# A graph layer's second aggregation with the operands of its matmuls exchanged, and gate logits on VectorE

## The chip, the cores and the metric

The kernel runs on one core of a Trainium2 chip. A core has TensorE (PE in the profile, with its weight loads as PEld), VectorE (DVE), ScalarE (ACT), GpSimd (POOL) and SyncE (SP); TensorE writes its results to PSUM (this kernel takes it in tiles of up to 512 fp32 values per partition, called banks here), and the other engines bring them to SBUF. The metric is the device time of one execution in microseconds (us), lower is better; the time before is the median of three runs.

## The reference: what is computed

6250 nodes with 256 features. `x` is normalised per row to `xn`. Three things are added to `x`: a graph network of two convolutions on `xn`, a linear attention on `xn`, and then, on the normalised sum, a mixture of experts with 8 experts of which each row uses 2. What matters here:

```python
def _graph_conv(x, edges, W0, b0, W1, b1):
    agg = segment_sum(x[src], dst, N_NODES) / deg[:, None]     # deg: edges into a node, at least 1
    return x @ W0 + b0 + agg @ W1 + b1
...
x = x + graph_network(xn) + linear_attention(xn)
x_flat = _layernorm(x)
gate_logits = x_flat @ Wg + bg + bias                          # 256 x 8
topk_vals, topk_idx = jax.lax.top_k(gate_logits, 2)
topk_w = softmax(topk_vals)
out = x + sum over the two chosen experts of topk_w * expert(x_flat)
```

The second convolution multiplies by its weight first and aggregates afterwards: the sum over a node's neighbours runs over rows of 256 values.

## The kernel before

Nodes are cut into NB = 49 blocks of 128 rows, and blocks into NGRP = 13 groups of T = 4 (the last has one block). Aggregation is a product with the adjacency matrix, built tile by tile. A step (g, j) in `steps` takes the edges from block j into the blocks of group g: 13 x 49 = 637 steps. `sent[:, j]` holds block j's rows to be summed, as a high and a low part (`k` = 0 and 1) in the fp32r format, 2 x 256 values per row.

Stages, in order of time:

1. Edges are sorted into `place`, while the rows of `x` are normalised.
2. The first pass (`aggregate`): for each step the adjacency tile is built from one-hots (L649, L668), copied to SBUF in fp32r (L671) and in bf16 (L679), and the latter is written to `adjd` in DRAM. `products` (L619 to L628) multiplies.
3. A dense stage makes `btab` (all that is added to a row besides the second aggregation) and the new `sent`.
4. **The second pass** (L931 to L1113), where the change lies.
5. The experts: 105 tiles of 128 rows (L1170 to L1286).

In the second pass each step needs the tile of adjacency in fp32r. SP reloads it from `adjd` in batches of JL = 7 steps (`reload`, L804, tile `many`, two buffers), and `widen` (L940) casts one step's part, on ScalarE in odd steps (L946) and on VectorE in even ones (L948), to one of five buffers of `adj2`. Then `products` issues four matmuls: stationary is one half (c) of the high or low rows, 128x128, moving is the adjacency, 128x512. So the sums, two banks per group, have a feature per partition and a node per column.

When a group's 49 steps are done, `gate(g)` (L951 to L1095) works on its four blocks. It is a generator in pieces; each `next(running)` issues one piece between steps of the next group, so that its work lies beside that group's matmuls. Its pieces, in order:

- load `btab` rows (L956), copy the two sums to `agT` (L959 on VectorE, L960 on ScalarE);
- per block: two transposes (L970) give rows again, L972 multiplies by 1/degree and adds `btab`; then the row's mean and variance (L975, L976);
- the standard deviation on ScalarE (L978), its reciprocal (L980), the normalised rows (L983), and GpSimd's copies of them (L986 to L988);
- transposes of the rows into `yT` (L994, copies L996), 16 matmuls with the gate's weight `wg` (L1005), and the bias (L1007): the logits `lg`;
- the two best experts and their weights (L1014 to L1055), with two small matmuls that count places (L1046, L1048), and the places (L1057 to L1079);
- GpSimd writes the rows to the experts' `lists` (L1085).

PE, VectorE and ScalarE execute their instructions in the order of the program here (`manual_schedule`); SP and GpSimd are left to a scheduler. The order is set by the loop at L1097: with AH = 4, the cast of step t stands before the products of step t - 4.

The constants of the gate are loaded at L895 to L900 by SP: `wg`, then `bg2`, which VectorE adds (L900).

Of the kernel before, what the change touches and what calls it, by code (L numbers as in the profile page):

```python
# [18 lines left out]
P = 128  # L19
# [14 lines left out]
def bcast_rows(ap, n):  # L34

    return bass.AP(tensor=ap.tensor, offset=ap.offset, ap=[[0, P], [1, n]])
# [3 lines left out]
def tile_gps_layer(ctx: ExitStack, tc: tile.TileContext, a, out):  # L40
# [578 lines left out]
    def products(pg, sums, adj, g, j):  # L619

        n = len(blocks(g))
        if j == 0:
            sums[g] = [pg.tile([P, T * P], F32, name=f"sum{c}") for c in range(DC)]
        for c in range(DC):
            for k in range(2):
                nc.tensor.matmul(sums[g][c][:, :n * P], sent[:, j, k, c * P:(c + 1) * P],  # L626
                                 adj[:, :n * P], start=(j == 0 and k == 0),
                                 stop=(j == NB - 1 and k == 1))  # L628
# [265 lines left out]
    gc = ctx.enter_context(tc.tile_pool(name="gate", bufs=1))  # L894
    wg = gc.tile([P, DC, NE], F32, name="wg")  # L895
    nc.sync.dma_start(wg, a["Wg"].rearrange("(c p) e -> p c e", p=P))
    bg2 = gc.tile([P, 2, NE], F32, name="bg2")
# [33 lines left out]
    with ExitStack() as p3:  # L931
        wk = p3.enter_context(tc.tile_pool(name="work3", bufs=2))
        ap = p3.enter_context(tc.tile_pool(name="adj2", bufs=5))
        pg = p3.enter_context(tc.tile_pool(name="pg2", bufs=2, space=PSUM))
        ps = p3.enter_context(tc.tile_pool(name="ps3", bufs=2, space=PSUM))
        py = p3.enter_context(tc.tile_pool(name="py3", bufs=2, space=PSUM))
        p3.enter_context(tc.manual_schedule(engines={ENG.PE, ENG.DVE, ENG.Activation}))
        adjs, sums = {}, {}

        def widen(t):  # L940
# [8 lines left out]
            adjs[t] = adj  # L949

        def gate(g):  # L951

            bs = blocks(g)
            n = len(bs)
            bt = wk.tile([P, T, D], F32, name="bt3")
            nc.sync.dma_start(  # L956
                bt[:, :n], btab[bs[0] * P:(bs[-1] + 1) * P, :].rearrange("(t p) d -> p t d", p=P))
            agT = wk.tile([P, DC, T * P], F32, name="agT", bufs=1)
            nc.vector.tensor_copy(agT[:, 0, :n * P], sums[g][0][:, :n * P])  # L959
            nc.scalar.copy(agT[:, 1, :n * P], sums[g][1][:, :n * P])  # L960
            yield
            yield
# [3 lines left out]
            rs = wk.tile([P, T], F32, name="rs3")  # L966
            for i, b in enumerate(bs):
                pt = py.tile([P, 512], F32, name="py")
                for c in range(DC):
                    nc.tensor.transpose(pt[:, c * P:(c + 1) * P], agT[:, c, i * P:(i + 1) * P],  # L970
                                        ident)
                nc.vector.scalar_tensor_tensor(bt[:, i], pt[:, :D], rdeg[:, b:b + 1], bt[:, i],  # L972
                                               op0=OP.mult, op1=OP.add)
                yield
                nc.vector.bn_stats(st[:, i, :], bt[:, i])  # L975
                nc.vector.bn_aggr(mv[:, i, :], st[:, i, :])  # L976
                yield
# [11 lines left out]
            yield  # L989
            yT = wk.tile([P, DC, T * P], F32, name="yT", bufs=1)  # L990
            for c in range(DC):
                tp = ps.tile([P, T * P], F32, name="tp")
                for i in range(n):
                    nc.tensor.transpose(tp[:, i * P:(i + 1) * P], rows[:, i, 0, c * P:(c + 1) * P],  # L994
                                        ident)
                nc.scalar.copy(yT[:, c, :n * P], tp[:, :n * P])  # L996
                yield
            yield


            lg = wk.tile([P, T, NE], F32, name="lg")
            pl = py.tile([P, 512], F32, name="py")
            for i in range(n):
                for c in range(DC):
                    nc.tensor.matmul(pl[:, i * NE:(i + 1) * NE], yT[:, c, i * P:(i + 1) * P],  # L1005
                                     wg[:, c, :], start=(c == 0), stop=(c == DC - 1))
            nc.vector.tensor_tensor(lg[:, :n], pl[:, :n * NE].rearrange("p (t e) -> p t e", e=NE),  # L1007
                                    bg[:, None, :].to_broadcast([P, n, NE]), op=OP.add)
            yield
            top = wk.tile([P, 2, T], F32, name="top")  # L1010
# [85 lines left out]

        AH = 4  # L1097
        running = iter(())
        for t in range(len(steps) + AH):
            if t < len(steps):  # L1100
                if steps[t][1] % JL == 0 and steps[t] not in loaded:
                    reload(t)
                widen(t)
            next(running, None)
            if t >= AH:
                g, j = steps[t - AH]
                products(pg, sums, adjs.pop(t - AH), g, j)
                if j == NB - 1:
                    for _ in running:
                        pass  # L1110
                    running = gate(g)
        for _ in running:
            pass  # L1113
# [210 lines left out]
```

## Time and profile before

| what | value |
|---|---|
| median of 3 runs | 2676.82 us (2675.69 to 2680.96) |
| the profiled execution's own time | 2674.58 us |
| its span, first to last instruction | 2672.8 us |
| mean granted clock of TensorE | 0.939 of full speed |
| busy in the span: PE, DVE, ACT, POOL | 92%, 59%, 36%, 13% |
| second pass: first matmul of L626, last matmul of L626 | 1555.2 us, 2191.9 us |
| busy from 1609 to 1660 us (51 us): PE, DVE, ACT, POOL | 51.0, 22.6, 18.9, 9.5 us |
| granted clock there | 1.00 |

A line such as `L948 DVE CAST adj<-many ... x319 | 135.8, 427 | 318.2 <-PE sum L626 254.8` says: the instructions of line 948 on VectorE, 319 of them, write `adj` from `many`; together 135.8 us busy, 427 ns each on average; before them the engine stood idle for 318.2 us in all, and 254.8 of it ended when TensorE had finished something at L626. In an order of time, a line gives the start, the length, the engine and line, and how many instructions were merged; the length of a merged row reaches to the end of its last instruction, so a pitch is the difference of two starts divided by the count. Matmuls are pipelined, so their durations overlap.

### The profile page before, as it was taken

What the parts mean: (1) busy time and instruction counts of PE and PEld (TensorE: products, weight loads), DVE (VectorE), ACT (ScalarE), POOL (GpSimd) and SP (SyncE); (2) the same over time, 40 slices, a digit from 0 to 9 for tenths busy, and PEclk for the clock granted to TensorE, in tenths of its full rate; (3) what the DMA queues carried; (4) which work ended last, traced back from release to release, by engine and by line L of the source; (5) the groups of instructions that cost most, each with busy time, mean ns of one, the idle gap of its engine ahead of it and who ended that gap; (6) DMA issues with size and microseconds to landing.
All of it is one profiled execution on the core that took longest, in us unless ns stands there. A gap on an engine that the chain in (4) does not pass through costs nothing. (4 is left out here: it accounts for less than half of the span.)

```text
span 2672.8 us, 41922 instructions
## 1 busy us (share of the span) xinstructions
PE 2452.5 (92%) x13030; PEld 1815.2 (68%) x13030; DVE 1587.8 (59%) x4247; ACT 951.0 (36%) x2476; POOL 344.6 (13%) x375
## 2 busy tenths in 40 slices
PE   3666769999999999989999989999999987999998
PEld 2455547777777777766677768888888874777665
DVE  5999888888888888721111124444434434666665
ACT  1332225555555555511111123334334322323332
POOL 0000000000000000000000011121121122454444
PEclk7777779999999999979999989999999978999999
DMA  2111613333333333222111154445454433223333
GB/s 75 52 51 52 209 54 109 108 107 107 107 107 107 105 110 108 86 66 83 55 56 55 50 208 150 165 161 168 156 166 162 150 120 96 77 76 103 105 112 96
DMA packets 227535, 286.75 MB, mean 107 GB/s; under 512 B 51798, under 2 KB 199937, under 8 KB 227046
## 3 DMA queue, kind: packets, MB, share of 16 engines
q1 hardware_dynamic: 204386, 241.06, 28.1%
q0 software_dynamic: 17072, 34.33, 3.8%
q10 hardware_dynamic: 5844, 8.58, 0.9%
q8 instruction: 107, 1.75, 0.3%
q14 instruction: 126, 1.03, 0.1%
HBM read 151.43 MB, written 147.10 MB: 112 GB/s over the span
## 5 line engine op out<-in xcount | busy, mean ns | idle before, releaser
L626 PE MATMUL sum<-adj,sent 128*128 128x512 f32 (+1 forms) x5096 | 1332.4, 403 | 10.2 <-DVE blank L918 5.9
L626 PEld LDWEIGHTS sum<-adj,sent 128*128 128x128 f32 x5096 | 907.9, 196 | 161.4 <-issue 6.3
L671 ACT ACTIVATE adj<-pt 128x512 fp32r<-128x512 f32 (+1 forms) x637 | 365.7, 574 | 337.2 <-PE pt L668 335.8
L649 DVE TENSOR_TENSOR oh<-iota,place 128x1024 bf16<-128x1024 bf16 (+1 forms) x686 | 426.7, 628 | 0.3 <-PE pt L668 0.2
L679 DVE CAST kept<-adj 128x512 bf16<-128x512 f32 (+1 forms) x637 | 262.1, 411 | 114.9 <-ACT adj L671 106.6
L946 ACT CAST adj<-many 128x512 fp32r<-128x512 bf16 (+1 forms) x318 | 188.8, 595 | 385.9 <-PE sum L626 345.1
L948 DVE CAST adj<-many 128x512 fp32r<-128x512 bf16 (+1 forms) x319 | 135.8, 427 | 318.2 <-PE sum L626 254.8
L668 PE MATMUL pt<-oh 128*128 128x128 bf16 x2548 | 261.5, 224 | 2.4 <-DVE oh L649 1.8
L668 PEld LDWEIGHTS <-oh 128*128 128x128 bf16 x2548 | 151.1, 99 | 161.8 <-DVE oh L649 131.3
L1226 PEld LDWEIGHTS po<-w2e,hT 128*128 128x128 f32 x840 | 159.4, 190 | 67.3 <-issue 26.3
L1206 PE MATMUL pm<-w1e,yT 128*128 x420 | 200.2, 599 | 1.8 <-DMA row<-lists 1.3
L1226 PE MATMUL po<-w2e,hT 128*128 x840 | 198.5, 379 | 1.0 <-ACT hT L1218 1.0
L1230 ACT ACTIVATE res<-res,row 128x256 f32<-128x256 f32 x105 | 53.3, 508 | 301.3 <-DVE res L1229 152.0
L453 PE MATMUL rt<-carry,route 128*128 128x100 bf16 x931 | 81.8, 265 | 84.5 <-DVE carry L440 65.3
L907 POOL IOTA home_i<- 128x8 int32 x1 | 0.1, 128 | 1158.5 <-DVEq L702 1158.5
L453 PEld LDWEIGHTS <-route 128*128 128x128 bf16 x931 | 73.1, 132 | 94.7 <-issue 84.5
L1085 POOL DMA_INDIRECT lists<-rows,place_i x98 | 97.2, 991 | 298.5 <-DVE rows L1077 265.1
L1262 POOL DMA_INDIRECT out_dram<-both,at x105 | 106.0, 1009 | 161.5 <-DVE both L1260 158.7
L872 DVE TENSOR_TENSOR bt<-bt,pb 128x256 f32<-128x256 f32 x49 | 20.6, 421 | 174.1 <-PE pb L870 174.1
L671 ACT ACTIVATION_READ_ACCUMULATOR adj<-pt 128x1 f32 x637 | 123.9, 194 | 0.0
L1247 POOL DMA_INDIRECT got<-ybuf,at x105 | 108.1, 1030 | 84.5 <-issue 33.0
L1209 DVE TENSOR_TENSOR hb<-pm,b1c 128x512 f32<-128x512 f32 x105 | 72.7, 692 | 64.2 <-PE pm L1206 62.0
(253 smaller groups left out, 2557.4 us busy)
## 6 DMA issues: line engine op xcount, KB each, us to landing
adjd<-kept SPq DMA_DIRECT2D x588, 128.0 KB
many<-adjd SPq DMA_DIRECT2D x84, 896.0 KB
row<-lists SPq DMA_DIRECT2D x105, 130.5 KB
ybuf<-xn SPq DMA_DIRECT2D x1, 13440.0 KB
ybuf<-res SPq DMA_DIRECT2D x105, 128.0 KB
xn<-in_x_dram SPq DMA_DIRECT2D x12, 512.0 KB
xnT_d<-xnT ACTq DMA_DIRECT2D x12, 512.0 KB
xnT<-xnT_d SPq DMA_DIRECT2D x12, 512.0 KB
```

The source lines that it names most:

```text
L453: nc.tensor.matmul(pl[:, r], routes[q // 4][:, q % 4, :, r], carry[:, q - q0, :, :, r], start=(q == 0), stop=(q == Q - 1))
L626: nc.tensor.matmul(sums[g][c][:, :n * P], sent[:, j, k, c * P:(c + 1) * P], adj[:, :n * P], start=(j == 0 and k == 0), stop=(j == NB - 1 a ...
L649: nc.vector.tensor_tensor(oh, iota2[:, None].to_broadcast([P, m, P, 2]), place[:, j, v0:v0 + m, None, :].to_broadcast([P, m, P, 2]), op=OP ...
L668: nc.tensor.matmul(cols, o[:, :, r], o[:, :, 1 - r], start=(m == 0), stop=(m + 1 == len(todo)))
L671: nc.scalar.activation(adj[:, :n * P], pt[:, :n * P], AF.Copy, accum_out=degp[:, j, g:g + 1])
L679: nc.vector.tensor_copy(kept[:, :n * P], adjs[t][:, :n * P].bitcast(F32))
L946: nc.scalar.copy(adj[:, :n * P], from_)
L948: nc.vector.tensor_copy(adj[:, :n * P], from_)
L1206: nc.tensor.matmul(pm, yT[:, c], w1e[:, bass.ds(e, 1), c, :].rearrange("p o f -> p (o f)"), start=(c == 0), stop=(c == DC - 1))
L1226: nc.tensor.matmul(po, hT[:, f], w2e[:, bass.ds(e, 1), f, :].rearrange("p o d -> p (o d)"), start=(f == 0), stop=(f == EC - 1))
L1247: ga = nc.gpsimd.indirect_dma_start(out=gots[t % 4], out_offset=None, in_=ybuf, in_offset=bass.IndirectOffsetOnAxis(ap=outs[t][1][:, 0:1], ...
L1262: st = nc.gpsimd.indirect_dma_start(out=out, out_offset=bass.IndirectOffsetOnAxis(ap=at[:, 1:2], axis=0), in_=both, in_offset=None, bounds ...
```

## The change

In the second pass the stationary operand becomes one 128x128 block of the adjacency tile, and the moving operand is the 512 values of block j's high and low rows together. A product gives one block's sums with a node per partition, the high rows' sum in the left 256 columns and the low rows' sum in the right ones: one PSUM bank per block, four per group, where two banks served a group before. `pg2` has six banks now, and the pool `ps3` is gone.

A new function `received` issues a step's products in place of `products`. During a group's first step (j = 0) it issues only blocks 0 and 1, and in the second step (HOLD = 2) these two and then blocks 2 and 3 of both steps. It also loads the group's `btab` rows in the first step.

`gate` no longer has `agT`: eight scalar_tensor_tensor add the two halves of each block's sum, times 1/degree, to the `btab` rows, and they are issued at once behind the last products of the group. `yT` is gone too: the logits are made on VectorE by eight multiply-and-sum instructions per block, one per expert, over 256 values; two of them are a piece. `wg` holds the whole weight on each partition (2048 values), by a load that repeats it for all 128. AH is 3.

```diff
-    wg = gc.tile([P, DC, NE], F32, name="wg")
-    nc.sync.dma_start(wg, a["Wg"].rearrange("(c p) e -> p c e", p=P))
+    wg = gc.tile([P, D, NE], F32, name="wg")
+    nc.sync.dma_start(wg.rearrange("p d e -> p (d e)"),
+                      bcast_rows(a["Wg"].rearrange("d e -> (d e)"), D * NE))
...
-        pg = p3.enter_context(tc.tile_pool(name="pg2", bufs=2, space=PSUM))
-        ps = p3.enter_context(tc.tile_pool(name="ps3", bufs=2, space=PSUM))
+        pg = p3.enter_context(tc.tile_pool(name="pg2", bufs=6, space=PSUM))
...
+        HOLD = 2
+        def received(t):
+            g, j = steps[t]
+            n = len(blocks(g))
+            if j == 0:
+                bts[g] = wk.tile([P, T, D], F32, name="bt3")
+                nc.sync.dma_start(
+                    bts[g][:, :n], btab[g * T * P:(g * T + n) * P, :].rearrange("(t p) d -> p t d", p=P))
+                sums[g] = []
+            todo = [(t, i) for i in range(n if j >= HOLD else min(n, 2))]
+            if j == HOLD - 1:
+                todo += [(s, i) for i in range(2, n) for s in range(t - HOLD + 1, t + 1)]
+            for s, i in todo:
+                js = steps[s][1]
+                if js == 0:
+                    sums[g].append(pg.tile([P, 2 * D], F32, name="sum"))
+                nc.tensor.matmul(sums[g][i], adjs[s][:, i * P:(i + 1) * P],
+                                 sent[:, js].rearrange("p k d -> p (k d)"),
+                                 start=(js == 0), stop=(js == NB - 1))
...
         def gate(g):
...
-            agT = wk.tile([P, DC, T * P], F32, name="agT", bufs=1)
-            nc.vector.tensor_copy(agT[:, 0, :n * P], sums[g][0][:, :n * P])
-            nc.scalar.copy(agT[:, 1, :n * P], sums[g][1][:, :n * P])
-            yield
+            bt = bts.pop(g)
+            for i, b in enumerate(bs):
+                for k in range(2):
+                    nc.vector.scalar_tensor_tensor(bt[:, i], sums[g][i][:, k * D:(k + 1) * D],
+                                                   rdeg[:, b:b + 1], bt[:, i], op0=OP.mult,
+                                                   op1=OP.add)
             yield
...
-            for i, b in enumerate(bs):
-                pt = py.tile([P, 512], F32, name="py")
-                for c in range(DC):
-                    nc.tensor.transpose(pt[:, c * P:(c + 1) * P], agT[:, c, i * P:(i + 1) * P],
-                                        ident)
-                nc.vector.scalar_tensor_tensor(bt[:, i], pt[:, :D], rdeg[:, b:b + 1], bt[:, i],
-                                               op0=OP.mult, op1=OP.add)
-                yield
+            for i in range(n):
                 nc.vector.bn_stats(st[:, i, :], bt[:, i])
                 nc.vector.bn_aggr(mv[:, i, :], st[:, i, :])
                 yield
...
-            yT = wk.tile([P, DC, T * P], F32, name="yT", bufs=1)
-            for c in range(DC):
-                tp = ps.tile([P, T * P], F32, name="tp")
-                for i in range(n):
-                    nc.tensor.transpose(tp[:, i * P:(i + 1) * P], rows[:, i, 0, c * P:(c + 1) * P],
-                                        ident)
-                nc.scalar.copy(yT[:, c, :n * P], tp[:, :n * P])
-                yield
-            yield
...
             lg = wk.tile([P, T, NE], F32, name="lg")
-            pl = py.tile([P, 512], F32, name="py")
-            for i in range(n):
-                for c in range(DC):
-                    nc.tensor.matmul(pl[:, i * NE:(i + 1) * NE], yT[:, c, i * P:(i + 1) * P],
-                                     wg[:, c, :], start=(c == 0), stop=(c == DC - 1))
-            nc.vector.tensor_tensor(lg[:, :n], pl[:, :n * NE].rearrange("p (t e) -> p t e", e=NE),
-                                    bg[:, None, :].to_broadcast([P, n, NE]), op=OP.add)
-            yield
+            for i in range(n):
+                for e in range(NE):
+                    nc.vector.tensor_tensor_reduce(
+                        out=bt[:, i], in0=rows[:, i, 0, :D], in1=wg[:, :, e], scale=1.0,
+                        scalar=bg[:, e:e + 1], op0=OP.mult, op1=OP.add, accum_out=lg[:, i, e:e + 1])
+                    if e % 2:
+                        yield
...
-        AH = 4
+        AH = 3
...
-                products(pg, sums, adjs.pop(t - AH), g, j)
+                received(t - AH)
                 if j == NB - 1:
                     for _ in running:
                         pass
                     running = gate(g)
+                    next(running)
```

## Prediction

> **What bounds the kernel now.** I read the table of 40 slices first, then the busy time by stretches, then the waits of the second pass, then the order of time on PE and on VectorE inside one group. The second pass runs from 1555 us, the first matmul of L626 after the dense stage, to 2191.9 us. First the costliest groups (out<-in, count | busy us, mean ns | idle before, and what ended it):
>
> ```profile
> L626 PE MATMUL sum<-adj,sent 128*128 128x512 f32 (+1 forms) x5096 | 1332.4, 403 | 10.2 <-DVE blank L918 5.9
> L946 ACT CAST adj<-many 128x512 fp32r<-128x512 bf16 (+1 forms) x318 | 188.8, 595 | 385.9 <-PE sum L626 345.1
> L948 DVE CAST adj<-many 128x512 fp32r<-128x512 bf16 (+1 forms) x319 | 135.8, 427 | 318.2 <-PE sum L626 254.8
> L671 ACT ACTIVATION_READ_ACCUMULATOR adj<-pt 128x1 f32 x637 | 123.9, 194 | 0.0
> ```
>
> Both casts wait for PE to free a buffer, and PE waits almost for nothing: TensorE is the bound. The 403 ns are no cost per matmul, since matmuls overlap; their pitch is read from the order of time on PE over one group (start, length, count):
>
> ```profile
> 1858.53 0.40 PE L970 MATMUL py<-ident,agT 128*128 128x128 f32 x2
> 1858.68 2.10 PE L626 MATMUL sum<-adj,sent 128*128 128x512 f32 x8
> 1860.62 0.38 PE L970 MATMUL py<-ident,agT 128*128 128x128 f32 x2
> ...
> 1872.47 0.60 PE L994 MATMUL tp<-ident,rows 128*128 128x128 f32 x4
> 1872.83 1.19 PE L626 MATMUL sum<-adj,sent 128*128 128x512 f32 x4
> ...
> 1876.17 1.85 PE L1005 MATMUL py<-wg,yT 128*128 128x8 f32 x16
> 1877.87 11.44 PE L626 MATMUL sum<-adj,sent 128*128 128x512 f32 x48
> 1889.14 0.19 PE L1046 MATMUL py<-both,after 128*128 128x32 bf16 x1
> 1889.18 0.18 PE L1048 MATMUL py<-ahead,onesb 128*128 128x32 bf16 x1
> 1889.21 18.91 PE L626 MATMUL sum<-adj,sent 128*128 128x512 f32 x80
> 1907.96 0.66 PE L970 MATMUL py<-ident,agT 128*128 128x128 f32 x2
> ```
>
> From 1889.21 to 1907.96 are 80 matmuls, so one is 0.2345 us and a step of four 0.938. A group's 196 are 46.0 us. The starts of L970 in groups ten apart (1611.26 and 2106.05) give 49.48 us per group. The other 3.5 us are gate(g)'s own PE work, of which L1046 and L1048 (0.08) stay.
>
> **What goes.** agT's transposes (L970), yT's transposes (L994), the logit matmuls (L1005) and their copies: 3.42 us of PE per group. Gates 0 to 10 run inside full groups, so 11 x 3.42 = 37.6 us. The new products are again four matmuls of 512 columns and four weight loads per step, so I keep 0.2345. That operands trade places may shift the pitch: in the first pass the same four take 1.01 us (700.72 to 701.73), 0.2525 each. I hold this as a rival.
>
> **What comes on VectorE.** Per full group: eight scalar_tensor_tensor (STT) in place of two halves of agT's eviction and four STT, and 32 multiply-and-sums (TTR, 256 elements, two fp32 SBUF inputs, a scalar operand, a sum written out). VectorE is busy 20 us of 50, so on average there is room; the order decides. Each step takes a cast (every second one on VectorE) and one piece of the gate; during the 32 TTRs a piece is two TTRs. The adjacency has five buffers, so VectorE cannot work more than four to five steps ahead.
>
> The pitch p of a TTR decides. Rows that bear on it:
>
> ```profile
> L1258 DVE SCALAR_TENSOR_TENSOR both<-row,got x105: 471/479/485, 2243.0 to 2667.2; 128x256 f32<-128x256 f32 x105
> L1152 DVE TENSOR_TENSOR diag<-ident,spec x1: 424/424/424, 2207.6 to 2207.6; 128x256 f32<-128x256 f32 x1
> L918 DVE MEMSET blank<- x1: 59/59/59, 1555.0 to 1555.0; 128x1 f32 x1
> ...
> 1621.32 0.74 DVE L983 TENSOR_SCALAR rows<-bt,mv,rs 128x256 f32<-128x256 f32 x2
> ...
> 2202.70 0.17 DVE L1036 TENSOR_TENSOR both<-pick 128x8 bf16<-128x8 f32 x1
> 2202.93 0.06 DVE L1040 MEMSET both<- 128x4 uint32 x1
> ```
>
> Two independent L983 (0.41 each) take 0.74: neighbours overlap by 0.08. L1040 overwrites what L1036 wrote and starts 0.06 after its end; other dependent neighbours start 0.03 to 0.04 after. All eight TTRs of a block write the same scratch row bt[:, i], so I count 0.04 of wait. Low end: a plain product that overlaps, 0.424 - 0.08 = 0.34. High end: STT 0.479, plus the separate read of a sum that ScalarE shows behind L671 (0.194), plus 0.04, is 0.71. I take STT plus the cheapest VectorE instruction that writes one value per partition (0.059) plus 0.04: **p = 0.58**, because STT has the same operands and the engine is VectorE, not ScalarE.
>
> The weight is read with a step of 32 bytes. Nearest rows: L305, whose int32 input alternates in steps of 76 bytes, takes 313 ns for 304 elements, as L302 does on a plain run, so I add nothing; L152 (34 elements in steps of 100 bytes, 192 ns) is 22 ns longer than L156 (49 elements in a row, 170 ns), at most some 0.9 ns per element, which would be 0.23 us per TTR, p = 0.81.
>
> The Trainium skill (SBUF — State Buffer, Door 1, on 16-byte lines) speaks against the change: each access that crosses into a new line pays a penalty, and here every access does. If that doubled the time per element, p would be an estimated 0.85 and the sum below +125 us; L305 against L302 shows no such price.
>
> **The sum inside a group**, from the end of its predecessor's last matmul, on VectorE: STTs start at -0.5 (they need a finished bank), in four pairs, dependent within a pair: 4 x 0.52 + 3 x 0.40 + 0.40 = 3.7, done at 3.2. Six casts at 0.35: 2.1. Four bn_stats with bn_aggr at 0.63: 2.5. Wait for the square root on ScalarE (table load 1.28 and 0.30, less a cast beside it): 1.3. Reciprocal 0.2, four rows at 0.33: 1.3. That is 10.6 when TTRs begin. Eight pairs of steps follow, each 4p + 0.35. The cast of step 30 is thus ready at 13.4 + 32p, and PE wants it at 29 x 0.938 = 27.2. PE's stall is 32p - 13.8, at least some 0.9 (the cast behind the STTs is late every second group, by 0.85; one bank 0.1; the root on ScalarE before its cast 0.3). With p = 0.58: 4.76 us against 3.42 saved, a net loss of 1.34 a group, 11 x 1.34 = +14.7.
>
> The casts queued behind TTRs are what PE waits for; HOLD covers the evictions, since two spare banks take 4 x 0.2345 = 0.94 us of matmuls and the first pair of STTs is done by 0.5. POOL's copy of rows (L986, 1.04 us) now runs beside TTRs and not transposes; I count nothing for it, or one microsecond a group if it blocks VectorE.
>
> **Group 12** (one block) took 2154.2 to 2191.9, 37.7 us, at 196 short matmuls; now PE needs 49 x 0.2345 = 11.5 and gate(11) is the longer: 3.7 + 2.8 stats + 1.6 root + 1.9 rows + 32p + 6.0 for L1014 to L1077 + 25 casts at 0.18 = 20.5 + 32p = 39.1: +1.4. **Tail**, gate(12): now 13.3 us from the last sum to L1119 (2205.26). Without transposes two STTs 1.05, then 3.24 to rows, 8p, and 4.97 as before: 8p - 4.0 = +0.6.
>
> **Start.** wg grows from 8 KB to 1 MB on SP's queue, ahead of bg, the rows of btab and reloads of many; L900 on VectorE waits for bg, with casts behind it. By stretches (PE, PEld, DVE, ACT, POOL busy, clock, DMA share, GB/s):
>
> ```profile
> 1560.00:1566.00 6.00, 6.00 (x28) 4.82 (x27) 1.28 (x3) 2.23 (x4) 0.17 (x1) 1.00 1.05 398
> 1566.00:1574.00 8.00, 4.27 (x19) 3.10 (x17) 0.30 (x1) 0.58 (x2) 0.00 (x0) 0.92 1.03 401
> ```
>
> Transfers are full here and PE waits 3.9 us for many. One more MB at 400 GB/s is 2.6 us; L900's own delay falls before that wait and is hidden, 0 to 5 in all. The btab load, moved from a gate's begin to step 0, is the same bytes and is not awaited earlier than the STTs; if late, it would hold VectorE (0 to 2 us a group). AH of 3 in place of 4 costs nothing beyond the sum, since buffers, not the order, limit the lead.
>
> Total: 14.7 + 1.4 + 0.6 + 2.6 = +19.3; in general 392p - 207.8, so break-even is p = 0.53. The profiled execution took 2674.58 (span 2672.8), the median is 2.24 above: 2676.8 + 19.3 = **2696 us**.
>
> **Rivals.**
> 1. TensorE stays the bound and it gets faster. If p is 0.45 or less, only the 0.9 stall remains: 11 x (0.9 - 3.42) - 2.8 - 0.4 + 2.6 = -28; at p = 0.50, -12. Middle: -22, 2655. For: VectorE has 30 us of 50 free. Against: TTRs sit in 16 steps of 15 us, where 8 casts and 32 TTRs take 2.8 + 32p. It decides below p = 0.53.
> 2. TTR far dearer (a separate read like ScalarE's, or the strided weight): p = 0.71 to 0.81, +71 to +110; 2765.
> 3. The change doesn't keep the pitch of matmuls: 0.2525 adds 0.018 x 2156 = 39 us on PE, of which the stalls hide a part: 2676.8 + 39, about 2716.
> 4. The two sides cancel, p 0.516 to 0.544, within 5 us.
>
> **Chances.** Forecast 0.45, rival 1 0.28, rival 2 0.12, rival 3 0.05, rival 4 0.10. This kernel's measurement can tell about 0.2% (5.4 us) from no change. Faster 0.28, within 0.10, slower 0.62. Signs differ, so the likeliest case's own range stands beside: p from 0.545 to 0.71, 2682 to 2748. The range reaches down to p = 0.34 (11 x -2.52 - 6.3 - 1.3 + 2.6 = -33, cut to -30) and up to 0.71 (+71): 2647 to 2748.
>
> **What would show it.** L970, L994, L1005 gone; sums' pitch in a run without TTRs 0.2345; PE idle before L626 ended by DVE's or ACT's cast of adj, some 4 to 5 us per group; TTR rows at 0.48 and a pitch near 0.58; casts in the stretch of TTRs no longer waiting for PE. Groups of 46 to 47 us instead of 49.48 would prove rival 1. A wrong lead (five buffers, 10.6 us before TTRs) by 1 us shifts 11 us in the total.

## The result and the profile after

| kernel | median | range | runs | against before |
|---|---|---|---|---|
| before | 2676.26 us | 2667.4 to 2680.96 | 4 | |
| after | 2765.55 us | 2756.95 to 2771.2 | 4 | 1.0343, 95% interval 1.031 to 1.0377 |

The changed kernel is 3.4% slower. The forecast was 2696 us in a range of 2647 to 2748: the sign held, the size did not, and the time lies outside the range, at the 2765 us of the second rival. The profiled execution took 2767.56 us (span 2765.8, granted clock 0.939 as before), 93.0 us more in span. In the changed kernel line 970 is the new product, L981 the scalar_tensor_tensors, L998 the normalised rows, L1009 the multiply-and-sums (in the trace CUSTOM_DVE_ANT_0) and L1089 the scatters into the lists.

The costliest groups of the changed kernel, in the columns of those of before:

```profile
L970 PE MATMUL sum<-sent,adj 128*128 128x512 f32 x2401 | 607.5, 407 | 114.3 <-DVE adj L948 110.8
...
L946 ACT CAST adj<-many 128x512 fp32r<-128x512 bf16 (+1 forms) x318 | 187.1, 595 | 464.1 <-PE sum L970 434.7
...
L1009 DVE CUSTOM_DVE_ANT_0 bt<-rows,wg,bg 128x256 f32<-128x256 f32 x392 | 287.0, 735 | 9.7
...
L948 DVE CAST adj<-many 128x512 fp32r<-128x512 bf16 (+1 forms) x319 | 129.6, 408 | 134.5 <-PE sum L970 105.2
```

TensorE, which waited for almost nothing before, now stands idle for 114 us, and nearly all of it ends with VectorE's cast. ScalarE's cast waits more than before: it isn't the late one. A multiply-and-sum takes 735 ns on average. The same groups on VectorE alone, with shapes kept apart, show a second instruction of the same line:

```profile
L1009 DVE CUSTOM_DVE_ANT_0 bt<-rows,wg,bg 128x256 f32<-128x256 f32 x392 | 287.0, 735 | 9.7
...
L1009 DVE DVE_READ_ACCUMULATOR2_ANT lg<- 128x1 f32 x392 | 33.2, 85 | 0.0
```

The order of time on VectorE, in group 3, where the multiply-and-sums begin (start, length):

```profile
1734.82 0.42 DVE L948 CAST adj<-many 128x512 fp32r<-128x512 bf16 x1
1735.15 1.52 DVE L1009 CUSTOM_DVE_ANT_0 bt<-rows,wg,bg 128x256 f32<-128x256 f32 x1
1736.60 0.07 DVE L1009 DVE_READ_ACCUMULATOR2_ANT lg<- 128x1 f32 x1
1736.71 0.74 DVE L1009 CUSTOM_DVE_ANT_0 bt<-rows,wg,bg 128x256 f32<-128x256 f32 x1
...
1738.94 0.44 DVE L948 CAST adj<-many 128x512 fp32r<-128x512 bf16 x1
```

The read of the sum lies under the end of its multiply-and-sum. The next casts start at 1738.94 and 1742.20: four multiply-and-sums and a cast are 3.25 us, so with 0.35 for the cast p = 0.725. The first one of a group is twice as long as the others. On TensorE, the same stretch:

```profile
1713.33 14.49 PE L970 MATMUL sum<-sent,adj 128*128 128x512 f32 x60
1728.24 13.35 PE L970 MATMUL sum<-sent,adj 128*128 128x512 f32 x56 [0.42 <-DVE adj L948]
1742.68 2.14 PE L970 MATMUL sum<-sent,adj 128*128 128x512 f32 x8 [1.09 <-DVE adj L948]
1745.95 2.13 PE L970 MATMUL sum<-sent,adj 128*128 128x512 f32 x8 [1.13 <-DVE adj L948]
```

TensorE runs on at the old pitch (1728.24 to 1741.59 is 56 matmuls) until its lead of five buffers is used up, and from there it does eight matmuls, two steps, for each pair of casts: 3.25 us in place of 1.88.

Where the 93.0 us of span came from, by the ends of the groups' last matmuls in both traces:

| stretch | before | after | difference |
|---|---|---|---|
| start of the program to the end of group 0 | 1609.6 | 1614.6 | +5.0 |
| groups 1 to 11, each | 49.49 | 55.96 | +71.2 in all |
| group 12 | 38.0 | 41.3 | +3.3 |
| last sum to the ends of the lists (L1119, now L1124) | 13.3 | 26.8 | +13.6 |
| the rest, with the experts | | | -0.2 |

For the experiments below, the group period is read from the starts of the counting matmul (L1046; L1050 in the changed kernel) in groups ten apart: 49.50 us before, 56.04 us after.

### The profile page after: what moved, and what is told of

It reads as the page before. It is cut to its first block, busy times and chain, and to the rows that moved or that the text cites. A ratio compares the mean times of both kernels' runs of the same rounds, so it can differ in the third digit from the quotient of the medians.

```text
span 2765.8 us, 41580 instructions
## 1 busy us (share of the span) xinstructions
PE 2428.0 (88%) x12491; PEld 1745.8 (63%) x12491; DVE 1859.4 (67%) x5054; ACT 930.8 (34%) x2437; POOL 347.8 (13%) x375
## 5 line engine op out<-in xcount | busy, mean ns | idle before, releaser
L626 PE MATMUL sum<-adj,sent 128*128 128x512 f32 (+1 forms) x2548 | 725.1, 409 | 0.0
L970 PE MATMUL sum<-sent,adj 128*128 128x512 f32 x2401 | 607.5, 407 | 114.3 <-DVE adj L948 110.8
L970 PEld LDWEIGHTS sum<-sent,adj 128*128 128x128 f32 x2401 | 448.1, 191 | 269.5 <-DVE adj L948 153.1
L626 PEld LDWEIGHTS sum<-adj,sent 128*128 128x128 f32 x2548 | 435.0, 195 | 51.0
L1009 DVE CUSTOM_DVE_ANT_0 bt<-rows,wg,bg 128x256 f32<-128x256 f32 x392 | 287.0, 735 | 9.7
L948 DVE CAST adj<-many 128x512 fp32r<-128x512 bf16 (+1 forms) x319 | 129.6, 408 | 134.5 <-PE sum L970 105.2
L1089 POOL DMA_INDIRECT lists<-rows,place_i x98 | 97.2, 991 | 492.4 <-DVE rows L1081 385.5
L1097 POOL DMA_DIRECT2D w1e<-in_W1e_dram x8 | 5.8, 729 | 1157.7 <-DMA btab<-bt 1157.5
```

Source lines behind the costliest of these rows:

```text
L948: nc.vector.tensor_copy(adj[:, :n * P], from_)
L970: nc.tensor.matmul(sums[g][i], adjs[s][:, i * P:(i + 1) * P], sent[:, js].rearrange("p k d -> p (k d)"), start=(js == 0), stop=(js == NB - 1))
L1009: nc.vector.tensor_tensor_reduce(out=bt[:, i], in0=rows[:, i, 0, :D], in1=wg[:, :, e], scale=1.0, scalar=bg[:, e:e + 1], op0=OP.mult, op1= ...
```

## The experiments

The theory after the result, A: a multiply-and-sum costs 0.725 and not 0.58 because it steps through the weight by 32 bytes. Against it stood B, that the sum output or the two fp32 inputs are dear in themselves, and C, that other parts (the first half of the change, the load of the weight) carry much of the loss.

**The weight in a row.** `wg` is held with an expert's 256 values side by side; everything else is the changed kernel.

```diff
-    wg = gc.tile([P, D, NE], F32, name="wg")
+    wg = gc.tile([P, NE, D], F32, name="wg")          # loaded from the transposed weight
...
-                        out=bt[:, i], in0=rows[:, i, 0, :D], in1=wg[:, :, e], scale=1.0,
+                        out=bt[:, i], in0=rows[:, i, 0, :D], in1=wg[:, e], scale=1.0,
```

> The changed kernel with the gate's weight held transposed, one expert's 256 values side by side, so that each multiply-and-sum reads its weight in a row and not in steps of 32 bytes. Theory A, the step makes the instruction 735 ns: it falls to about 480 ns (the STT row of L1258), a pitch of 0.48 in place of 0.725, by my sum 392 x (0.48 - 0.725) = -96 us against the changed kernel, some 2670 us. Theory B, the instruction itself is slow, whatever its step: 735 ns again and 2766 us within 10.

Measured: 2677.9 us, ratio to before 1.0008 (0.9992 to 1.0025; each ratio here is to executions of the kernel before taken along with the run). The group period is 48.51 us. VectorE in the stretch:

```profile
1721.64 0.42 DVE L948 CAST adj<-many 128x512 fp32r<-128x512 bf16 x1
1721.98 0.48 DVE L1009 CUSTOM_DVE_ANT_0 bt<-rows,wg,bg 128x256 f32<-128x256 f32 x1
...
1722.50 0.48 DVE L1009 CUSTOM_DVE_ANT_0 bt<-rows,wg,bg 128x256 f32<-128x256 f32 x1
...
1723.97 0.42 DVE L948 CAST adj<-many 128x512 fp32r<-128x512 bf16 x1
```

0.48 in place of 0.74; four and a cast are 2.33 us, so p = 0.495. The order of the weight's values alone is worth 88 us of the 89: A holds, B and C don't explain the loss. With the step gone and nothing else, VectorE's logits are no better than TensorE's were.

**Seven forms of the same work, in one kernel.** Per block, the eight logits were replaced by one each of the instructions below; the logits of this kernel are not the reference's.

> A look at one instruction's length. The changed kernel with the eight multiply-and-sums of a block replaced by different forms (the logits are then not the reference's): multiply-and-sum with the weight in steps of 32 bytes, with the weight in a row, the same with a constant as start value in place of a pointer, the same with both inputs bf16; a plain product in steps and in a row; an STT in steps. Theory A (the step costs): forms in steps are some 250 ns above the same form in a row, so product in steps 680, in a row 424. Theory B (the summing instruction costs): all multiply-and-sums of fp32 735 whatever the step, products 424 and STT 480 in both. If the two fp32 inputs are the cause within B, the bf16 form is near 480.

The groups on VectorE (count 49 each):

```profile
L1014 DVE CUSTOM_DVE_ANT_0 bt<-rows,wg,bg 128x256 f32<-128x256 f32 x49 | 37.0, 756 | 1.7
L1032 DVE SCALAR_TENSOR_TENSOR bt<-rows,bg,wg 128x256 f32<-128x256 f32 x49 | 35.5, 724 | 1.7
L1029 DVE TENSOR_TENSOR bt<-rows,wg 128x256 f32<-128x256 f32 x49 | 33.0, 673 | 1.7
L1017 DVE CUSTOM_DVE_ANT_0 bt<-rows,wg,bg 128x256 f32<-128x256 f32 x49 | 23.8, 485 | 1.7
L1026 DVE CUSTOM_DVE_ANT_0 bt<-bt,wg,bg 128x256 bf16<-128x256 bf16 x49 | 23.6, 482 | 0.9
L1031 DVE TENSOR_TENSOR bt<-rows,wg 128x256 f32<-128x256 f32 x49 | 20.8, 425 | 0.9
L1021 DVE CUSTOM_DVE_ANT_0 bt<-rows,wg 128x256 f32<-128x256 f32 x49 | 20.7, 422 | 0.9
```

The first three step by 32 bytes, the rest read in a row. A plain product pays 673 - 425 = 248 ns for the step, a scalar_tensor_tensor 724 against the 479 of L1258 before, 245. So the step costs some 0.97 ns per element whatever the instruction. The sum costs nothing in the instruction itself (422 with a constant start value, 425 for the plain product); a start value from memory costs 485 - 422 = 63 ns; bf16 inputs and output (482) save nothing.

**The first half alone.** Sums with a node per partition as in the change; the rows are still transposed on TensorE and multiplied with the small `wg` there.

> Only the first half of the change: sums with a node per partition, HOLD and AH as in the change, but the logits on TensorE as before (yT, 16 small matmuls, a weight load of 8 KB). If the multiply-and-sums carry the whole loss: TensorE is the bound again, 46.0 + 0.9 (yT) + 1.7 (logits) + 0.1 = 48.7 us a group against 49.5, -9 us over 11 groups, about -10 in group 12, perhaps +6 in the tail: 2660 to 2672 us. Rival, the exchanged operands lose by themselves (casts late behind the evictions, another pitch): over 2690 us, with PE waiting for adj outside any logits.

Measured: 2667.48 us, ratio 0.9969 (0.9951 to 0.9988): 8 to 9 us faster than before by the medians. So the exchange of operands is a gain, and the second half loses some 98 us against it. The total came out as expected, the group did not: its period is 49.26 and not 48.7, so the groups gave some 2 us in place of 9. Most of the gain is at group 12 (28.1 us in place of 38.0), where gate(11) is the longer: a gate's counting matmul now comes 5.5 us earlier in its group (in group 1 at 1635.46 in place of 1641.82). The tail takes 5.6 us of it back.

**The last gate's rows elsewhere.** The table shows 13.6 us at the tail. In the changed kernel VectorE waits there for the scatters of gate(11), which read the only buffer of `rows`:

```profile
2271.52 1.00 DVE L981 SCALAR_TENSOR_TENSOR bt<-sum,rdeg,bt 128x256 f32<-128x256 f32 x2 [0.89 <-PE sum L970]
2287.00 0.41 DVE L998 TENSOR_SCALAR rows<-bt,mv,rs 128x256 f32<-128x256 f32 x1 [11.94 <-DMA lists<-rows,place_i]
```

```diff
-            rows = wk.tile([P, T, 2, R], F32, name="rows", bufs=1)
+            if n == T:
+                rows = wk.tile([P, T, 2, R], F32, name="rows", bufs=1)
+            else:                       # group 12 has one block: use the free part of its bt
+                rows = bt.rearrange("p t d -> p (t d)")[:, D:D + 2 * R].rearrange(
+                    "p (t k r) -> p t k r", t=1, k=2)
```

> The changed kernel, but the last group's one block writes its normalised rows to free space of its btab tile instead of the single rows tile. In the trace of the changed kernel VectorE waits 11.9 us there for the scatters of the group before. Theory: this wait is on the path, the time falls by 11 to 12 us to about 2754. Rival: it is covered by what comes after (the experts wait for those scatters in any case), and the time stays at 2762 to 2766.

Measured: 2757.35 us, ratio 1.031 (1.0279 to 1.0341), 8 us below the changed kernel's median; in the traces the stretch from the last sum is 14.9 us in place of 26.8, so the wait is shown. Then the same edit on the first half alone:

> The first half alone (sums with a node per partition, logits on TensorE as before), and the last group's rows in the free part of its own bt tile instead of the single rows tile. Theory that gate(12) waits some 12 us for gate(11)'s scatters in this kernel too: the tail becomes shorter by 8 to 12 us, the time goes from the 2667.5 of the first half alone to 2655 to 2660. Rival, that the wait is hidden here because TensorE carries the logits and gate(11) ends early: within 2 us of 2667.5.

Measured: 2661.8 us, ratio 0.9944 (0.9922 to 0.9966): 5.7 us less than without the edit. The wait is there too, but shorter (7.7 us, since gate(11) ends earlier); my 2655 to 2660 was too much.

**GpSimd's copy beside the first multiply-and-sum.** L1001 copies the rows while VectorE begins the logits. First I only put it behind them in the program:

```diff
-            nc.gpsimd.tensor_copy(rows[:, :n, 1, :D], rows[:, :n, 0, :D])
...
                         scalar=bg[:, e:e + 1], op0=OP.mult, op1=OP.add, accum_out=lg[:, i, e:e + 1])
                     if e % 2:
                         yield
+            nc.gpsimd.tensor_copy(rows[:, :n, 1, :D], rows[:, :n, 0, :D])
```

> The changed kernel with GpSimd's copy of rows moved behind the multiply-and-sums in program order. Theory that this copy slows the first multiply-and-sum of each group (1.52 us against 0.73) through contention: the first one takes 0.73 again, a group is shorter by about 0.8 us, the total by 8 to 10 us from 2765.6, to about 2756. Rival, that the first one is long for another reason (first read of rows or of the weight): it stays at 1.5 us and the time within 2 us of 2765.6. The copy now stands in front of the scatters by some microseconds less, which the tail could pay: up to 1 us.

Measured: 2769.63 us (2765.1 to 2771.83), ratio 1.0357 (1.033 to 1.0385). This told nothing of the theory: no semaphore held the copy, and it still started when the rows were there. The first line is GpSimd, the second VectorE, each from its engine's order of time:

```profile
1733.68 1.17 POOL L1013 COPY rows<-rows 128x1024 f32<-128x1024 f32 x1 [2.36 <-DVE rows L998]
```

```profile
1733.87 1.52 DVE L1008 CUSTOM_DVE_ANT_0 bt<-rows,wg,bg 128x256 f32<-128x256 f32 x1
```

So I held it back by letting GpSimd read the last logit first:

```diff
+            nc.gpsimd.tensor_copy(rows[:, 0, 1, :1], lg[:, n - 1, NE - 1:NE])
+            nc.gpsimd.tensor_copy(rows[:, :n, 1, :D], rows[:, :n, 0, :D])
```

> The changed kernel with GpSimd's copy of rows really later: ahead of it GpSimd reads the last logit, so that the copy can't start before the last multiply-and-sum (in the kernel where it only stood later in the order it still ran beside the first one, since nothing held it). Theory that the copy slows the multiply-and-sum that runs beside it: the first of each group takes 0.73 us, a group is shorter by 0.8 us, the time 8 to 10 us below the changed kernel, 2756. Rival, that the first one is long of itself: it stays at 1.5 us and the time at 2765 to 2770.

Measured: 2764.27 us, ratio 1.0334 (1.0309 to 1.036). The first multiply-and-sum of the group:

```profile
1734.60 0.73 DVE L1008 CUSTOM_DVE_ANT_0 bt<-rows,wg,bg 128x256 f32<-128x256 f32 x1
```

The mechanism is shown: 1.52 us beside the copy, 0.73 without it. Its price isn't what I expected: the group period falls only from 56.04 to 55.71, and the total by 1.3 us, within what the measurement can tell. Every second group is some 0.6 us shorter, the others not at all; what takes the gain there stays open.

**The weight's load, later in the program.** The 1 MB at step 28, and in a second kernel at step 44:

```diff
-    nc.sync.dma_start(wg.rearrange("p d e -> p (d e)"),
-                      bcast_rows(a["Wg"].rearrange("d e -> (d e)"), D * NE))
...
                 widen(t)
+            if t == 28:                 # 44 in the second kernel
+                nc.sync.dma_start(wg.rearrange("p d e -> p (d e)"),
+                                  bcast_rows(a["Wg"].rearrange("d e -> (d e)"), D * NE))
```

> The changed kernel with the load of the weight (1 MB) issued at step 28 of the second pass, behind the first loads of the adjacency, instead of ahead of them. Theory that this load delays the start of the second pass by the about 5 us seen: group 0 ends 3 to 5 us earlier, the time is 2761 to 2763 in place of 2765.6. Rival, that the begin is late for other reasons (order of the five buffers, first sums): within 1 us.

> The changed kernel with the weight's load (1 MB) at step 44 of the second pass, where the transfers are only 40% busy, instead of step 28, where group 0 ended only 1.8 us earlier. Theory that its bytes cost their transfer time in any place of the first 30 us, in which transfers are full, and nothing behind it: group 0 ends 3 to 5 us earlier than in the changed kernel, the time 2761 to 2763. Rival, that the start isn't lost to this load: within 1 us of 2765.6.

Measured: 2764.65 us (ratio 1.0324, 1.0294 to 1.0354) and 2767.92 us (1.035, 1.0324 to 1.0376): no difference from the changed kernel's 2765.55. But the load was not later in either. SP's instructions are left to a scheduler, and it issued this one at the beginning of the pass again, as in the changed kernel (1555.85), ahead of the pass's first reload of `many` (both lines are of the second kernel; the first has 1556.17 and 1560.89):

```profile
1558.20 0.43 SPq L1107 DMA_DIRECT2D wg<-in_Wg_dram  x1
1562.93 0.32 SPq L808 DMA_DIRECT2D many<-adjd  x1
```

So these two kernels don't test the theory. Other traces bear on it. From its first matmul to its last, group 0 takes 54.4 us before, and 54.4 and 54.5 us in the two kernels with the first half alone, whose weight is loaded with 8 KB. It takes 57.1 us in the changed kernel, and 55.4 to 57.5 in all kernels that load the 1 MB and `b1c` there. In the two kernels further down that load `b1c` (2 MB of the 6.3 MB on GpSimd's queue in this stretch) behind the second pass, it takes 52.7. What is loaded beside group 0 thus costs time there, and the forecast of 2.6 us for the 1 MB fits the 2.7 between the kernels, though no run moved this load alone. The cost has two parts. The changed kernel has two waits for `many`, 2.42 and 2.45 us, where the kernel before has one of 3.92; and behind each wait, as at the beginning of the pass, TensorE does several matmuls at a pitch of 0.43 us (the granted clock is 0.65 from 1586 to 1590 us): 26 in the changed kernel, 18 before. The other 2.3 of the 5.0 us lie ahead of the pass, whose first matmul comes at 1555.2 before and at 1557.4 in the changed kernel. Most of that is a longer wait of TensorE just before this matmul: 5.9 to 6.2 us in the three kernels with the logits on TensorE, 7.4 to 8.2 in all with them on VectorE. What makes it longer stays open.

**All costs taken away.** The weight in a row, a constant start value (the bias added once per group in place of the copy to `l2`), GpSimd's copy later in the program (which, as above, doesn't hold it back: the first multiply-and-sum that it meets takes 1.14 us), the last rows in `bt`.

> The changed kernel with every cost found so far taken away: weight in rows of 256 in a row, constant start value 0 (bias added once per group in place of the copy into l2), GpSimd's copy behind the multiply-and-sums, the last group's rows in bt. The pitch p should be 0.43 (one with a constant start took 422 ns). By the sum of the prediction, a group's stall is then at its least, 0.9 us, against 3.42 us saved: 11 groups -28, group 12 20.5 + 32 x 0.43 - 37.7 = -3.4, tail -0.6, start +5: about 2650. If a cost that I haven't seen remains in the multiply-and-sums, the group period stays near the 48.4 us of the flat weight alone and the time is 2662 to 2668.

Measured: 2644.26 us, ratio 0.9883 (0.9859 to 0.9908): faster than before and 6 us under the expectation. TensorE is the bound again; one whole group and the start of the next:

```profile
1650.06 46.51 PE L970 MATMUL sum<-sent,adj 128*128 128x512 f32 x196
...
1696.47 14.49 PE L970 MATMUL sum<-sent,adj 128*128 128x512 f32 x60
```

196 matmuls without a break in 46.4 us (the counting matmul that follows starts at 1696.41); the next group has one break, of 0.42. The group period is 46.71. With the held-back copy besides, and the load at step 44 of the program (issued at 1556.8 us, so not late either):

> The version with a row-wise weight, constant start value and the last group's rows in bt (2644.3), and besides the held-back copy and the weight's load at step 44. TensorE is already its bound inside groups, so the copy should give little, 11 x at most 0.4; the load 2 to 5 us: 2637 to 2643. Rival, no difference within 2 us of 2644.

Measured: 2642.04 us, ratio 0.9871 (0.9847 to 0.9896), 2 us below the one above, which these runs can't tell from none. These are the best versions of the study, some 34 us below the kernel before.

**Order or total.** The prediction took the order of VectorE's instructions as the limit, casts queued behind multiply-and-sums. VectorE's total is a rival: it is busy 43.72 us in a group of 56.45. So I kept the dear multiply-and-sums and laid them over 24 steps in place of 16:

```diff
-                    if e % 2:
+                    if e % 4 != 2:
                         yield
```

> The changed kernel with its multiply-and-sums laid over 24 steps in place of 16 (one, one, two to a step). The theory of the prediction, that the order of VectorE's work sets the loss and not its total: with 0.725 us each, TensorE's stall is 10.6 + 32p + 12 x 0.35 - 37 x 0.938 = 3.3 us in a group in place of 32p - 13.8 = 9.4; with 0.8 us for the first one, some 6 us less in each of 11 groups: about 2700. Rival, that VectorE's total (some 45 us in a group of 46 on TensorE) is the bound: above 2740.

Measured: 2757.9 us, ratio 1.0312 (1.0286 to 1.0338); group period 55.05. Missed, above even the rival's bound of 2740, but for another reason. VectorE, by its own waits (total us, times, longest):

```profile
DVE rows L998 <- DMA lists<-rows,place_i: 73.0, 12, 13.0
```

In the changed kernel the same wait is 12.9 us, in 2 places. The gate now ends at its group's end, and the next gate finds the only `rows` buffer still read by the scatters: the tail's wait, in each group. In the stretch of multiply-and-sums TensorE's breaks had shrunk from 1.1 us to 0.2 to 0.4. The last two kernels give `rows` two buffers (the room comes from `b1c`, whose load moves behind the second pass), one with the spread order and one with the change's own:

> The multiply-and-sums over 24 steps as in the spread kernel, and two buffers for rows (room from b1c, whose load moves behind the second pass). Theory that the order of VectorE's work sets the loss, and that the spread kernel paid for it in a new wait (73 us on VectorE for the scatters that free the single rows buffer): that wait goes, a group takes 46.1 + 3.3 = 49.4 us plus 0.8 for the first multiply-and-sum where it isn't hidden, in place of 55.05; ten groups 50 to 55 us less, the tail some 8 less: 2690 to 2705. Rival, that VectorE's total is the bound and the wait only took the place of stalls that come back: a group stays above 53 us, the time above 2735.

> The changed kernel with two buffers for rows and b1c's load behind the second pass, its order unchanged: the control for the run above. A group stays at 56.0 us, since there it waits for no scatter; only the tail is shorter by some 12 us, of which b1c's load may take a part back: 2752 to 2762. If two buffers alone shortened the group, the spread order would deserve no credit.

Measured: 2695.3 us (ratio 1.008, 1.0058 to 1.0102), group period 50.74; and the control 2758.81 us (1.0306, 1.0266 to 1.0347), group period 56.59. One group of each, busy time of the engines (PE, PEld, DVE, ACT, POOL, granted clock, DMA share, GB/s), first the changed kernel, then the spread one with two buffers:

```profile
1713.33:1769.78 56.45, 48.25 (x201) 35.94 (x201) 43.72 (x142) 18.17 (x29) 9.48 (x11) 1.00 0.43 142
```

```profile
1695.94:1746.94 51.00, 48.25 (x201) 35.98 (x201) 43.11 (x142) 18.30 (x29) 9.53 (x11) 1.00 0.48 158
```

The same work on every engine, and 5.45 us less. Two buffers alone do nothing for the group; the spread order alone is worth 1 us; both together over 5 us a group. Against the control the order is worth 63.5 us, against the changed kernel 70. A small part is not the order's: in most groups of the spread kernel with two buffers GpSimd's copy is done before the first multiply-and-sum begins (0.75 us in place of 1.5), which held back by itself was worth 0.33 us a group. The order, not the total, is the limit, and it is shown.

## Why the prediction was wrong

Point by point, by its own steps:

- **TensorE's saving and pitch: right.** The lines named are gone, and the whole group without a break, 46.41 us for 196 matmuls, has a pitch of 0.237, 1% above the 0.2345 forecast. Rival 3 (0.2525) fell.
- **The rule for a group: right.** Saved 3.42, stall 32p - 13.8. With p as measured, 0.725, the group is 46.06 + 9.4 = 55.5, and 56.3 with the 0.8 of the first multiply-and-sum; seen 55.96. With 0.495 (weight in a row) 46.06 + 2.0 + 0.8 = 48.9, seen 48.5. With 0.43 it says that TensorE is the bound, at 46.06 + 0.9 = 47.0; seen 46.7. The break-even was put at 0.53; the row-wise kernel, at 0.495, still ties with before, since the waits of the start and the tail and the copy, which the sum had low or at nothing, are in it too.
- **p: this is the step that failed**, in the words "L305 ... takes 313 ns for 304 elements, as L302 does on a plain run, so I add nothing". The step adds 248 ns to 256 elements. The row chosen, L305, alternates between places 76 bytes apart and did not stand for it; the one set aside, L152 at "most some 0.9 ns per element", was the right price: it gave p = 0.81, measured 0.725, because the rest had been put too high (0.58 by the prediction, 0.495 measured in a row: the read of the sum, 0.085, hides under its neighbours). The term of 14.7 us was mis-sized: it measured 71.2, and of the 56.5 us between them 51 are the 0.145 us too little for 32 instructions in 11 groups.
- **The Trainium skill on the step.** The prediction weighed the Trainium skill (SBUF — State Buffer, Door 1), estimated p = 0.85 from it and set it aside for L305. The measurement sides with the rule, at 0.97 ns per element. Another page of the Trainium skill, which the prediction didn't use, has figures: the Vector Engine (DVE) Microarchitecture Reference, 5.2 (Measured stream behaviour on trn2, on the access granule), gives 1.054 ns per column for contiguous operands, 1.73 with one source hopping 4 KiB at every element and 2.50 to 2.51 with both sources, or the output alone, stepping 24 words. Estimated from these, 256 elements pay 0.17 to 0.37 us; the 0.248 measured here lies between.
- **GpSimd's copy: priced at "nothing for it, or one microsecond a group if it blocks VectorE".** It blocks it, by 0.79 us; but holding it back gave the group only 0.33. The Trainium skill (SBUF — State Buffer, Who interferes with whom) says that a VectorE instruction with two SBUF inputs and a GpSimd instruction that reads SBUF exclude each other, and that the one that begins first holds the other up. The trace agrees in the main: the copy ran from 1733.68 to 1734.85, and the multiply-and-sum beside it ended at 1735.39, 0.54 behind the copy's end; but the copy was slowed too, 1.17 us against 1.05 where it was held back.
- **Tail: +0.6 forecast, +13.6 seen.** I worked out the path of data through gate(12) and not the buffer that it writes into. `rows` is single, and a longer gate(11) moves its scatters against gate(12)'s first write. With the wait gone, the tail is 14.9, 1.0 above the forecast 13.9.
- **Group 12: +1.4 forecast, +3.3 seen.** The sign came from the right gate, the size by two errors against each other: with p as measured its sum is 20.5 + 23.2 = 43.7 us, +6.0, so its other terms were some 2.4 us too high.
- **Start: +2.6 forecast, +5.0 between the two traces.** Of these 2.7 lie inside group 0, as the mechanism given, 1 MB more on a full queue, would have it; the kernels with the small weight don't have them. The other 2.3 lie ahead of it, 1.9 of them in the wait before the pass's first matmul; their cause stays open.

The second rival named the mechanism ("the strided weight") and the time (2765) and got a chance of 0.12. That its time is met to 1 us is in part luck: with p as measured the prediction's sum gives +76, 2753 us, and most of the rest is the tail's wait for the scatters, which neither the forecast nor a rival had. Two of three hints pointed to it; one row was allowed to outweigh them, although its access pattern was not that of the change.

## What to carry to other kernels

On VectorE the layout of an operand is a cost of its own: before work is moved there, hold each operand so that its innermost run is contiguous, or add what the step costs, some 1 ns per element for the 32 bytes measured here. Where several engines feed one bound engine, look at what is queued in front of the feeding instruction and spread dear pieces over as many of its periods as there are, since the busy total need not be the limit. And a step that ends later pushes on every single-buffered tile that it reads: check when the next writer wants it, and that a thing moved later is held there by a dependency and not only by its place in the program: GpSimd's copy and the weight's load were both moved in the program and ran when they had run before.

## What the runs showed of the hardware

- An operand read by 32-byte steps costs 248 ns more for 256 fp32 values in a product (425 to 673), 245 in a scalar_tensor_tensor, and brings the usual multiply-and-sum from 0.48 to 0.74 us.
- A multiply-and-sum is two instructions, 422 ns and a read of 83 to 85 ns that overlaps its neighbours; a start value per partition in place of a constant adds 63 ns, and bf16 inputs and output save nothing (482 against 485).
- GpSimd's copy of 128x1024 values held a VectorE instruction with two SBUF inputs from 0.73 to 1.52 us.
